# A GRU over 128 steps: step 0's products of r ahead of step 1's, the bias products in front of them, and one set of GpSimd's sums a step earlier

## The chip, the cores and the metric

The kernel runs on one core of a Trainium2 chip. The metric is the device time of one execution in microseconds (us), taken as the median of three runs. Beside it stands one profiled execution, whose trace gives the start and the end of every instruction; the span is the time from its first to its last instruction.

The engines go by these names in the profile: PE is TensorE (matmuls; PEld its weight loads), DVE is VectorE, ACT is ScalarE, POOL is GpSimd, SP is SyncE, which here issues transfers only. SPq, ACTq and POOLq are transfers issued by these three engines.

## The reference

A gated recurrent unit over x (64 sequences, 128 steps, 512 inputs), with a start state of 64 x 512, and the input added to its output. All in float32.

```
def step(h, inp):
    x_t, prop = inp
    comb = concatenate([x_t, h], axis=-1)
    z = sigmoid(comb @ Wz + bz)
    r = sigmoid(comb @ Wr + br)
    comb2 = concatenate([x_t, r * h], axis=-1)
    h_cand = tanh(comb2 @ Wh + bh)
    h_new = (1.0 - z) * h + z * h_cand
    h_next = where(prop, tanh(h_new @ Wp + bp), h_new)
    return (h_next, h_new)
# prop holds at every fourth step but the last
# out = x + the h_new of all steps
```

Each weight matrix of the gates has 1024 rows: the first 512 meet x (the input weights, `wx` in the kernel), the last 512 meet h (the recurrent weights, `wh`). Wp has 512 rows.

## The kernel before, in words

The 64 sequences are worked on in two halves of 32. The state lies with four column blocks of 128 side by side in the partitions (`NQ = 4`, `V = 32`). Every matmul of the kernel uses a 32-column strip of TensorE, so four of them run beside each other.

There are two kinds of product. The recurrent ones (`gate`, tiles `rec_0`, `rec_1`, `rec_z`) need the state of the step before: r first, then z, then the candidate with r * h, then at every fourth step the propagation with Wp. The input products do not depend on the state and are put into the gaps of the recurrence as a queue of units (`put`, `fill`). One unit of the plain kind (`plain_unit`) is one 128-row block `k` of x times one gate's input weights, for both halves: eight matmul instructions. From step 4 on the input products are formed for four steps at a time from sums and differences of x and of the weights (`batch`), which takes fewer products and leaves additions to VectorE and GpSimd. GpSimd forms the sums of the weights (`sum_outer`, `sum_inner`) in the first four steps and the sums of x (`sum_raw12`, `sum_s12`, `sum_raw4` and so on) all along, adds the parts of the results (`pair_left`, `outer_1`, ...), and adds the state to x for the output (line 803).

The order of the work on each engine is the order of the program text: it is written out by hand and no scheduler changes it. Two generators, one for each half, are interleaved by a count of columns (`LAG`, at the end of the kernel). Each engine works through its own instructions in order and waits for the others by semaphores. SyncE, ScalarE and GpSimd also issue transfers, and these stand in the order of that engine's other work. The transfers of SyncE and ScalarE share eight completion counters: a transfer that takes a counter first waits for the last one that held it.

The change concerns the start. Its order before is this:

- Loads: x of step 0 (four pieces on SyncE and ScalarE), r's input weights in two halves (`load_wx(R, 0, 2)`, `load_wx(R, 2, K)`, SyncE), between them x of step 1 (ScalarE) and the three bias rows (GpSimd's queue, line 132), then z's and the candidate's input weights (SyncE, 1 MB each), x of step 2, the start state (GpSimd's queue, behind a small copy that waits for r's weights).
- TensorE: 48 products of zeros (`idle(48)`); two units of r for step 0; two units of r for step 1; the bias products (`spread`: a row of ones times the bias rows, which ScalarE then copies into `bias_x`); the other two units of r for step 0 and for step 1; then the units of z, of the candidate, of step 2, and the recurrence of step 0 with r's recurrent weights.
- VectorE transposes x of a step (`join_x`) before that step's units; ScalarE issues half of the loads of r's recurrent weights (`load_wh(R)`) behind its three copies of the bias products.

Later, GpSimd has this order around steps 2 and 3: the bias and the sum of the first pair behind r of step 2 (`pair_left(0, 1, 2)`), the sums of x for the steps 8 to 11 (`sum_raw12`, `sum_s12`), line 803 of step 2, then behind r of step 3 `pair_right(0, 1, 10)` and the four operations of `sum_inner(7, ...)` (lines 319 to 322), then behind step 3 `pair_left(1, 8, 9)` and `pair_right(1, 8, 11)` and the sums that follow, up to `sum_raw4` (tile `s4r`, lines 330 to 333).

Of the kernel before, what the change touches and what calls it, by code (L numbers as in the profile page):

```python
# [18 lines left out]
def kernel(  # L19
# [14 lines left out]
    nc = tc.nc  # L34
# [13 lines left out]
    R, Z, H_ = range(3)  # L48
# [39 lines left out]
    def part(q):  # L88
        return slice(q * V, (q + 1) * V)
# [22 lines left out]
    def load_step(t, engs=both_queues):  # L112
        for q in (0, 2, 1, 3):
            engs[q // 2].dma_start(
                out=xr[0][part(q), t], in_=x[:, t, ts(q, J)].rearrange("(h b) u -> b h u", h=S)
            )

    def load_wx(i, k0, k1):
        nc.sync.dma_start(
            out=wx[:, k0:k1, i, :],  # L120
            in_=gates_in[i][:D].rearrange("(p k) n -> p k n", k=K)[:, k0:k1],
        )
# [3 lines left out]
    bias_p = const.tile([P, S, J], F32, name="bias_p")  # L126
    new_xr(0)
    load_step(0)
    load_wx(R, 0, 2)
    load_step(1, (nc.scalar, nc.scalar))  # L130
    for i, b in enumerate((br, bh, bz)):
        nc.gpsimd.dma_start(out=bias_row[:, i, :], in_=b.rearrange("(o n) -> o n", o=1))
# [17 lines left out]
    def load_wh(i):  # L150
        load_w(wh[i], gates_in[i][D:], engs=both_queues)
# [36 lines left out]
    def quarters(v):  # L188
        return v.rearrange("p n (d c j) -> p c n d j", d=2, c=2)

    def spread(bank, rows, which):
        bank = bank.rearrange("p (i d j) -> p i d j", i=2, d=2)
        for h in range(S):
            for c in range(2):
                nc.tensor.matmul(
                    bank[part(2 * h + c), 0 : len(which)],
                    lhsT=ones,
                    rhs=quarters(bias_row[:, rows])[:, c],
                    start=True,
                    stop=True,  # L200
                )
        for j, i in enumerate(which):
            nc.scalar.copy(
                bias_x[:, :, :, i, :].rearrange("p n d u -> p d n u"),
                bank[:, j].rearrange("p d (n u) -> p d n u", n=C),
            )
# [4 lines left out]
    def idle(n):  # L211
        for i in range(n):
            nc.tensor.matmul(
                rec[i // NQ % 3].rearrange("p a d n -> p (a d n)")[part(i % NQ)],
                lhsT=zeros[:, :V],
                rhs=zeros,
                start=True,
                stop=True,
            )
# [39 lines left out]
    def join_x(g, i):  # L259
        if g * Q4 >= T:  # L260
            return
        if g not in xT:
            xT[g] = xtp.tile([P, Q4, C, P], F32, tag="xT", name=f"xT_{g}")
        src = xr[g] if g < FIRST else xs[g]
        nc.vector.transpose(
            out=xT[g][:, i].rearrange("p c (a h b) -> p h (c a) b", a=S, h=S),
            in_=src[:, i].rearrange("p h (e k) -> p h k e", k=K),
        )
# [14 lines left out]
    def inner(i, ka, na):  # L283
        return OPERAND[i](ka)[:, :, :, ts(na, J // 4)]

    def leftover(i):
        return din[:, i - 1] if i <= 3 else inner(i, 0, 1)
# [25 lines left out]
    def sum_inner(i, eng, gates=slice(0, 3)):  # L313
        def of(v):
            return v[:, :, gates]

        t = [of(tt[:, i - 1, n]) for n in range(3)]
        v = {ab: of(inner(i, *ab)) for ab in ((0, 0), (0, 1), (1, 0), (1, 1))}
        eng.tensor_sub(t[1], v[1, 1], v[0, 1])
        eng.tensor_add(t[0], t[1], v[0, 0])  # L320
        eng.tensor_sub(t[2], v[1, 0], t[0])
        eng.tensor_sub(of(leftover(i)), v[0, 1], v[0, 0])
# [88 lines left out]
    def put(units):  # L411
        for unit, cols, bank, end, read in units:
            queue.append((unit, cols, reader.get(bank, -1), end))
            for b in read:
                reader[b] = len(queue) - 1
# [38 lines left out]
    def plain(t, gates=(R, Z, H_)):  # L454
        order = [(e, k) for e in gates for k in range(K)]
        if t == Q4 - 1:
            order = [(e, k) for k in range(K) for e in gates]
        return [
            plain_unit(
                t,  # L460
                e,
                k,
                k == 0,
                *((lambda: add_bias(t, gates), gates) if t > 1 and (e, k) == order[-1] else ()),
            )
            for e, k in order
        ]
# [101 lines left out]
    def add(dst, a, b):  # L569
        nc.gpsimd.tensor_add(dst, a, b)  # L570

    def with_bias(g, i, v):
        m = M[g, i].rearrange("p b d g u -> p b (d g u)")
        v = v.rearrange("p d g u -> p (d g u)")
        nc.gpsimd.tensor_add(m, m, v.unsqueeze(1).to_broadcast([P, 2, 3 * J]))  # L575

    def c_block(g, a, nb):
        new_cp(2 * g + a)
        return flat(cp[2 * g + a][:, nb])

    def m_(g, i):
        return flat(M[g, i])
# [17 lines left out]
    def outer_u2(g):  # L600
        add(m_(g, 7), m_(g, 7), m_(g, 6))
# [7 lines left out]
    def pair_left(a, p1, p2, g=1):  # L609
        with_bias(g, p2, bias0)  # L610
        add(c_block(g, a, 0), m_(g, p1), m_(g, p2))

    def pair_right(a, p1, x_, g=1):
        with_bias(g, x_, bias_x[:, 1])
        add(c_block(g, a, 1), m_(g, p1), m_(g, x_))
# [11 lines left out]
    def both(n):  # L627
        for _ in range(n):
            for h in range(S):
                for _ in fill(1, h):  # L630
                    pass

    def now(units):
        put(units)
        both(len(units))

    first = {i: [plain(t, (i,)) for t in range(2)] for i in (R, Z, H_)}
    idle(48)
    join_x(0, 0)
    now(first[R][0][:2])  # L640
    join_x(0, 1)
    now(first[R][1][:2])
    spread(scratch[3], slice(0, 2), (R, H_))
    spread(scratch[1], slice(2, 3), (Z,))
    nc.gpsimd.tensor_sub(bias_d, bias_x[:, 1], bias0)
    load_wh(R)
    now(first[R][0][2:] + first[R][1][2:])
    for t in range(2):
        add_bias(t, (R,))
    for h in range(S):  # L650
# [65 lines left out]
    def behind_r(t, duo, u):  # L716
        odd = FIRST + 2 * duo + 1
        if t == 2:
            pair_left(0, 1, 2)
        elif t == 3:  # L720
            pair_right(0, 1, 10)
            sum_inner(7, nc.gpsimd)
        if t == 4:
            sum_inner(4, nc.gpsimd)
        if u == 0 and duo >= 1 and odd - 2 < LAST:
            outer_u2(odd - 2)
# [101 lines left out]
    def half(h):  # L828

        for t in range(T):  # L830
# [10 lines left out]
            if h == 1:  # L841
                behind_r(t, duo, u)
# [129 lines left out]
```

## Time and profile before

| what | us |
|---|---|
| median of three runs | 1269.39 |
| lowest, highest | 1267.61, 1269.46 |
| the profiled execution's own time | 1266.3 |
| its span | 1264.5 |
| TensorE busy | 1250.6 |
| GpSimd busy | 891.1 |
| ScalarE busy | 835.2 |
| VectorE busy | 803.9 |

A row of the trace in order of time has the start in us, the duration, the engine, the line of the kernel, the operation, what it writes and reads, the shapes, how many instructions the row merges, and in brackets how long the engine stood idle before it and what ended that. Matmuls are pipelined, so the duration of one is longer than the distance to the next. A row of stretches has the bounds, the length, the busy time of PE, PEld, DVE, ACT and POOL with their counts, the clock that TensorE was granted as a share of the full one, the mean busy share of the DMA engines, and the GB/s that they moved. A row of transfers has KB each and the median us from issue to landing. Line numbers are those of the kernel before.

### The profile page before, as it was taken

What the parts mean: (1) busy time and instruction counts of PE and PEld (TensorE: products, weight loads), DVE (VectorE), ACT (ScalarE), POOL (GpSimd) and SP (SyncE); (2) the same over time, 40 slices, a digit from 0 to 9 for tenths busy, and PEclk for the clock granted to TensorE, in tenths of its full rate; (3) what the DMA queues carried; (4) which work ended last, traced back from release to release, by engine and by line L of the source; (5) the groups of instructions that cost most, each with busy time, mean ns of one, the idle gap of its engine ahead of it and who ended that gap; (6) DMA issues with size and microseconds to landing.
All of it is one profiled execution on the core that took longest, in us unless ns stands there. A gap on an engine that the chain in (4) does not pass through costs nothing.

```text
span 1264.5 us, 60718 instructions
## 1 busy us (share of the span) xinstructions
PE 1250.6 (99%) x25960; PEld 1161.0 (92%) x25960; DVE 803.9 (64%) x2165; ACT 835.2 (66%) x2685; POOL 891.1 (70%) x1032
## 2 busy tenths in 40 slices
PE   8999999999999999999999999999999999999997
PEld 4798899999999999999999999999999999999875
DVE  4665666666666666666666666666666666666544
ACT  1566666666666666666666666666666666667665
POOL 3899767777776778767778677777767787677530
PEclk9999999999999999999999999999999999999999
DMA  8301111111121110211111211111111111111010
GB/s 234 95 22 45 44 51 49 40 37 53 36 53 41 48 51 22 53 53 37 53 28 45 53 44 45 42 47 37 52 39 51 44 29 53 53 36 36 15 40 19
DMA packets 113172, 60.82 MB, mean 48 GB/s; under 512 B 12776, under 2 KB 109288, under 8 KB 112904
## 3 DMA queue, kind: packets, MB, share of 16 engines
q1 hardware_dynamic: 110532, 54.71, 16.3%
q8 instruction: 205, 3.36, 1.1%
q10 hardware_dynamic: 2116, 2.10, 0.7%
q14 instruction: 63, 0.52, 0.1%
q0 software_dynamic: 256, 0.14, 0.1%
HBM read 40.11 MB, written 16.78 MB: 45 GB/s over the span
## 4 chain that ended last, share of the span: by engine, by line
PE 94%; POOL 2%; issue 1%; DMA 1%; ACT 1%; DVE 1%; SPq 0%; ACTq 0%; POOLq 0%; DVEq 0%
PE rec L223 42%; PE rec_z L223 16%; PE scratch_r L223 13%; PE scratch_q L223 10%; PE scratch_a L223 5%; PE scratch_x L223 4%; PE scratch_y L223 4%; DMA xr<-in_x_dram 1%; POOL cp L570 1%; POOL mb L575 1%; ACT rec_z L249 0%; SPq L813 0%; POOL xr L803 0%; ACT c L249 0%; DVE rec_z L884 0%
## 5 line engine op out<-in xcount | busy, mean ns | idle before, releaser
L223 PE MATMUL rec<-wh,rhT 128*32 128x256 f32 x4096 | 375.1, 379 | 0.0
L223 PE MATMUL rec<-wh,hT 128*32 128x256 f32 x3072 | 281.2, 379 | 1.7 <-DVE hT L252 1.7
L223 PE MATMUL rec_z<-wh,hT 128*32 128x256 f32 x3072 | 281.5, 379 | 0.1
L223 PEld LDWEIGHTS rec<-wh,rhT 128*32 128x32 f32 x4096 | 249.6, 110 | 19.1 <-ACT scratch_r L249 0.5
L249 ACT ACTIVATE scratch_r<-rec 64x128 f32<-64x128 f32 x512 | 128.0, 250 | 133.9 <-PE rec L223 67.7
L399 ACT COPY rec<-cp 64x256 f32<-64x256 f32 x512 | 189.8, 371 | 21.5 <-DVE cp L437 2.0
L223 PEld LDWEIGHTS rec_z<-wh,hT 128*32 128x32 f32 x3072 | 192.1, 110 | 9.3 <-ACT rec_z L399 0.6
L223 PEld LDWEIGHTS rec<-wh,hT 128*32 128x32 f32 x3072 | 186.2, 110 | 14.6 <-ACT c L249 2.7
L249 ACT ACTIVATE rec_z<-rec_z 64x128 f32<-64x128 f32 x512 | 128.0, 250 | 97.8 <-PE rec_z L223 85.7
L249 ACT ACTIVATE c<-rec 64x128 f32<-64x128 f32 x512 | 138.9, 271 | 60.2 <-PE rec L223 48.8
L803 POOL TENSOR_TENSOR xr<-xr,h 128x256 f32<-128x256 f32 x127 | 92.9, 732 | 93.0 <-DVE h L893 93.0
L570 POOL TENSOR_TENSOR mb<-mb,mb 128x768 f32<-128x768 f32 x58 | 106.2, 1832 | 67.0 <-DVE mb L536 67.0
L570 POOL TENSOR_TENSOR cp<-mb,mb 128x768 f32<-128x768 f32 x76 | 139.0, 1829 | 8.1 <-DVE mb L536 4.4
L570 POOL TENSOR_TENSOR cp<-mb 128x768 f32<-128x768 f32 x46 | 84.3, 1832 | 56.8 <-ACT rec_z L399 55.4
L223 PE MATMUL scratch_r<-tw,s 128*32 128x192 f32 x928 | 120.9, 326 | 0.0
L509 ACT COPY cq<-scratch_q 128x384 f32<-128x384 f32 x212 | 102.0, 481 | 19.8 <-PE scratch_q L223 18.4
L526 DVE TENSOR_TENSOR cx<-scratch_r,cx 128x384 f32<-128x384 f32 x106 | 59.1, 557 | 85.8 <-PE scratch_r L223 67.9
L861 DVE SCALAR_TENSOR_TENSOR keep<-rec_z,h 128x256 f32<-128x256 f32 x96 | 40.7, 424 | 104.1 <-ACT rec_z L249 99.9
L223 PE MATMUL scratch_q<-tt,s 128*32 128x192 f32 x928 | 103.6, 326 | 0.0
L532 DVE TENSOR_TENSOR mb<-scratch_q,cx 128x384 f32<-128x384 f32 x106 | 59.0, 557 | 62.7 <-ACT cq L509 62.7
L845 DVE TENSOR_TENSOR rh<-scratch_r,h 128x128 f32<-128x128 f32 x192 | 56.0, 292 | 60.3 <-ACT scratch_r L249 60.3
L223 PE MATMUL rec<-wh,hpT 128*32 128x256 f32 x992 | 91.4, 379 | 0.1
(183 smaller groups left out, 3832.3 us busy)
## 6 DMA issues: line engine op xcount, KB each, us to landing
out_dram<-xr SPq DMA_DIRECT2D x249, 64.0 KB, 1.8
xr<-in_x_dram SPq DMA_DIRECT2D x248, 64.0 KB, 2.0
xs<-in_x_dram SPq DMA_DIRECT2D x240, 64.0 KB, 2.0
wx<-in_L_cond_Wr_dram SPq DMA_DIRECT2D x2, 512.0 KB, 5.0
wx<-in_L_cond_Wz_dram SPq DMA_DIRECT2D x1, 1024.0 KB, 7.1
wx<-in_L_cond_Wh_dram SPq DMA_DIRECT2D x1, 1024.0 KB, 8.2
wp<-in_L_cond_Wp_dram SPq DMA_DIRECT2D x4, 256.0 KB, 5.0
wh<-in_L_cond_Wr_dram SPq DMA_DIRECT2D x2, 256.0 KB, 9.9
```

The lines of the kernel that those rows point to most:

```text
L223: nc.tensor.matmul(ps[part(2 * h + c)], lhsT=left, rhs=rhs(c), start=start, stop=True, skip_group_check=True,)
L249: nc.scalar.activation(dst[ts(d, 2 * V)], gate_ps(i, h)[ts(h, 2 * V), d, :], func)
L399: nc.scalar.copy(gate_ps(i, h)[rows].rearrange("p d (c n) -> p d c n", c=C), G[t][rows, :, :, i, :].rearrange("p c d n -> p d c n"),)
L509: nc.scalar.copy(c[:, :nm], ps[:, :nm])
L526: nc.vector.tensor_add(T2[what][:, :nm], r_ps[:, :nm], T2[what][:, :nm])
L532: nc.vector.tensor_add(blocks(1, 1), runs(q_ps[:, :nm]), runs(T2[what][:, :nm]))
L570: nc.gpsimd.tensor_add(dst, a, b)
L575: nc.gpsimd.tensor_add(m, m, v.unsqueeze(1).to_broadcast([P, 2, 3 * J]))
L803: nc.gpsimd.tensor_add(xr[g][:, j], xr[g][:, j], h_new)
L845: nc.vector.tensor_mul(rh[:, h, :], r_, h_old[:, h, :])
L861: nc.vector.scalar_tensor_tensor(out=keep, in0=z, scalar=1.0, in1=h_old, op0=ALU.subtract, op1=ALU.mult)
```

## The change

In the loads, r's input weights come in three pieces instead of two: the first row block, the second, and the last two together. In TensorE's order there are 36 products of zeros instead of 48; the bias products come right behind them, ahead of all units of r; then come the four units of r for step 0, then the four for step 1. The loads of r's recurrent weights and GpSimd's `bias_d` stand between these two groups in the text. On GpSimd, the four operations of `sum_inner(7, ...)` stand behind r of step 2 instead of step 3. No operation other than the twelve products of zeros is removed, and the order on VectorE is the same as before.

```diff
     load_step(0)
-    load_wx(R, 0, 2)
+    load_wx(R, 0, 1)
+    load_wx(R, 1, 2)
     load_step(1, (nc.scalar, nc.scalar))
...
-    idle(48)
-    join_x(0, 0)
-    now(first[R][0][:2])
-    join_x(0, 1)
-    now(first[R][1][:2])
+    idle(36)
     spread(scratch[3], slice(0, 2), (R, H_))
     spread(scratch[1], slice(2, 3), (Z,))
+    join_x(0, 0)
+    now(first[R][0])
+    join_x(0, 1)
     nc.gpsimd.tensor_sub(bias_d, bias_x[:, 1], bias0)
     load_wh(R)
-    now(first[R][0][2:] + first[R][1][2:])
+    now(first[R][1])
...
         if t == 2:
             pair_left(0, 1, 2)
+            sum_inner(7, nc.gpsimd)
         elif t == 3:
             pair_right(0, 1, 10)
-            sum_inner(7, nc.gpsimd)
```

## The prediction

> **What bounds the kernel now.** I read the busy times first, then TensorE's start in order of time, its clock by stretches, the loads, and last GpSimd around the one wait of TensorE between start and end that is over 1 us.
>
> From the page:
> ```profile
> span 1264.5 us, 60718 instructions
> PE 1250.6 (99%) x25960; PEld 1161.0 (92%) x25960; DVE 803.9 (64%) x2165; ACT 835.2 (66%) x2685; POOL 891.1 (70%) x1032
> ```
> TensorE is busy for 1250.6 of 1264.5 us. An edit pays only where TensorE stands still or runs at a lower clock, and that is some fifteen microseconds in all.
>
> Its start in order of time (start, us, engine and line, what, count, [idle before, and what ended it]):
> ```profile
> 5.24 0.39 PE L213 MATMUL rec_z<-zeros 128*32 128x512 bf16 x4
> 6.83 1.07 PE L223 MATMUL scratch_q<-wx,xT 128*32 128x256 f32 x16 [1.20 <-DMA wx<-in_L_cond_Wr_dram]
> 9.38 1.07 PE L223 MATMUL scratch_a<-wx,xT 128*32 128x256 f32 x16 [1.49 <-DVE xT L265]
> 10.39 1.06 PE L195 MATMUL scratch_x<-tt,ones 1*32 1x512 f32 x8
> 11.27 0.94 PE L195 MATMUL scratch_r<-tt,ones 1*32 1x256 f32 x8
> ...
> 15.20 1.90 PE L223 MATMUL scratch_q<-wx,xT 128*32 128x256 f32 x32
> 16.93 1.90 PE L223 MATMUL scratch_a<-wx,xT 128*32 128x256 f32 x32
> 18.65 1.90 PE L223 MATMUL scratch_r<-wx,xT 128*32 128x256 f32 x32
> ```
> ```profile
> 24.70 1.93 PE L223 MATMUL rec<-wh,hT_init 128*32 128x256 f32 x28
> ```
> r's first units run at 6.83, after 1.20 of waiting for r's input weights; step 1's at 9.38, after 1.49 for its transposed x; z's at 15.20, the candidate's at 18.65, the recurrence from 24.70. From 15.20 to 16.93 32 instructions take 1.73 us: 0.43 per unit of 8 at full clock, so r's eight units are 3.45. The bias products are 0.88 (10.39 to 11.27) for the rows of 512 columns, so 0.44 for as many of 256: 1.32 together. What follows them is slower, and the stretches say why (PE, PEld, DVE, ACT, POOL busy, then the granted clock, DMA share, GB/s):
> ```profile
> 4.59:8.01 3.42, 2.11 (x36) 0.81 (x28) 0.87 (x1) 0.51 (x2) 0.00 (x0) 1.00 1.03 357
> 8.01:11.42 3.41, 2.04 (x28) 0.82 (x32) 0.63 (x1) 0.00 (x0) 1.52 (x3) 1.00 1.03 348
> 11.42:14.83 3.41, 3.41 (x40) 1.32 (x32) 0.42 (x1) 1.18 (x4) 0.99 (x1) 0.50 1.08 312
> ```
> ```profile
> 1257.28:1260.70 3.42, 1.33 (x20) 0.47 (x8) 1.60 (x5) 1.78 (x7) 0.72 (x1) 1.00 0.08 19
> 1260.70:1264.50 3.80, 0.00 (x0) 0.00 (x0) 0.00 (x0) 0.00 (x0) 0.00 (x0) 0.50 0.13 35
> ```
> From 11.42 to 14.83 the clock is 0.50: 1.7 us lost. The stretch before it was busy for 2.04 us; the one at the end that also precedes 0.50 for 1.33; the one that kept the clock for 2.11.
>
> **The change, part by part.**
>
> Fewer warm-up products. Twelve of 48 go. At the 0.43 us for eight that r's units show, twelve are 0.65, so they now end near 5.0 instead of 5.6 (5.24 + 0.39). Nothing waits for them, but the stretch from 4.59 to 8.01 becomes emptier, which comes below.
>
> Bias products first. They wait for the bias rows, which GpSimd's queue loads (issues, then KB each and us from issue to landing):
> ```profile
> 1.96 0.51 POOL L132 DMA_DIRECT2D tt<-in_L_cond_bh_dram  x1
> 2.46 0.48 POOL L132 DMA_DIRECT2D tt<-in_L_cond_bz_dram  x1
> ```
> ```profile
> tt<-in_L_cond_bh_dram POOLq DMA_DIRECT2D x1, 2.0 KB, 4.9
> tt<-in_L_cond_bz_dram POOLq DMA_DIRECT2D x1, 2.0 KB, 4.9
> ```
> Landings at 6.9 and 7.4. At 10.39 nobody noticed; now TensorE starts with them, at 6.9, and the wait for r's weights is replaced by one for the bias rows of the same length.
>
> The clock. From 4.59 to 8.01 the new kernel is busy for some 0.4 (warm-up) and 1.1 (from 6.9): 1.5 us, near the 1.33 that was followed by 0.50. So I take half clock from 8.01 to 11.42, in place of 11.42 to 14.83: the loss of 1.7 us moves and stays.
>
> r's units. The work ahead of z is 1.32 + 3.45 = 4.77, plus 1.7 for the clock: 6.9 + 6.5 = 13.4; with the 0.2 that the same sum misses today (9.38 + 3.9 + 1.7 = 15.0 against 15.20) z begins at 13.6, 1.6 us earlier. Step 1's x, ready by 9.38, is needed only near 11.7, so that wait of 1.5 is covered; if it were not, it would cost again what it costs now.
>
> The loads (SyncE's and ScalarE's issues; then us to landing):
> ```profile
> 4.60 0.66 SPq L119 DMA_DIRECT2D wx<-in_L_cond_Wz_dram  x1
> 8.31 0.54 SPq L119 DMA_DIRECT2D wx<-in_L_cond_Wh_dram  x1
> 12.26 0.80 ACTq L100 DMA_DIRECT2D wh<-in_L_cond_Wr_dram  x2
> ```
> ```profile
> wx<-in_L_cond_Wz_dram SPq DMA_DIRECT2D x1, 1024.0 KB, 7.1
> wx<-in_L_cond_Wh_dram SPq DMA_DIRECT2D x1, 1024.0 KB, 8.2
> ```
> ```profile
> wh<-in_L_cond_Wr_dram ACTq DMA_DIRECT2D x2, 256.0 KB, 9.6
> ```
> z's input weights land at 4.60 + 7.1 = 11.7, the candidate's at 8.31 + 8.2 = 16.5, r's recurrent ones by 12.26 + 0.4 + 9.6 = 22.3. One more load on SyncE is 0.4 us of issue there (half of 0.80 for two on ScalarE). It also shifts who waits for whom, since each load waits for an earlier one that held its completion counter: the last of r's three (half the weights) now waits where z's does today, until 4.60, and z's follows at 5.1. The engines are at a share of 1.03 in that stretch, so a later issue is mostly hidden behind packets already queued; I put 0 to 0.5 us on z's landing, 12.0, still before 13.6. The candidate's load waits for another piece of step 1's x: 8.7 in place of 8.31. The two loads of r's recurrent weights on SyncE now wait for z's landing and go out near 12.0; from there the same loads took ScalarE's queue 9.6 us, so 21.6 to 22.0, and they are needed at 24.70 less the gain, 23.6: covered. Those on ScalarE stand behind the three copies of the bias products, which now end near 9: issued at 9 instead of 12.26, into the time in which the candidate's weights move.
>
> Here lies the term that decides. TensorE could start the candidate at 13.6 + 3.45 = 17.0; the weights landed at 16.5 before. Rates around it:
> ```profile
> 9.00:13.00 4.00, 3.62 (x42) 1.23 (x46) 0.33 (x1) 1.02 (x3) 1.52 (x3) 0.80 1.03 359
> 13.00:16.00 3.00, 3.00 (x44) 1.57 (x40) 0.97 (x3) 0.74 (x2) 0.70 (x1) 0.69 1.11 206
> ```
> ScalarE's two loads are 0.52 MB. None of it ahead of the candidate's last byte: 16.5, no wait. All of it, at 206 GB/s: 2.5 us later, 19.0. I take the lower third, 0.8 us, since SyncE's own pair now stays out of that time: 17.3, so the candidate starts at 17.5 instead of 18.65. The start gains 1.1 us, between 1.6 and -0.4. Everything behind it shifts along, as long as GpSimd's own chain keeps up.
>
> GpSimd's sums. Four operations leave the place behind step 3's r for step 2's:
> ```profile
> 62.38 0.46 POOL L330 TENSOR_TENSOR s12r<-xT 128x128 f32<-128x128 f32 x1 [4.74 <-PE scratch_r L223]
> ...
> 71.96 1.00 POOL L319 TENSOR_TENSOR tt<-tw 128x384 f32<-128x384 f32 x1
> ...
> 76.07 1.84 POOL L575 TENSOR_TENSOR mb<-mb,bias_x 128x768 f32<-128x768 f32 x1
> ...
> 103.89 0.32 POOL L332 TENSOR_TENSOR s4r<-xT 128x64 f32<-128x64 f32 x1
> ```
> ```profile
> 73.89 0.55 DVE L536 TENSOR_TENSOR mb<-scratch_x,cq 128x384 f32<-128x384 f32 x1
> ```
> ```profile
> 102.83 0.36 PE L223 MATMUL scratch_a<-wx,xT 128*32 128x192 f32 x2
> 104.26 0.36 PE L223 MATMUL scratch_x<-tt,s4r 128*32 128x192 f32 x2 [1.07 <-POOL s4r L332]
> ```
> ```profile
> 62.38:104.21 41.83, 40.81 (x870) 37.43 (x862) 26.41 (x70) 25.80 (x82) 40.49 (x46) 1.00 0.17 41
> ```
> They last from 71.96 to 76.07, 4.1 us, and go into the hole of 4.74 before 62.38, where GpSimd waits for TensorE anyway. Behind 62.38 GpSimd is busy to s4r without a pause worth the name (busy for 40.49 of 41.83 us in the last row), so s4r could come 4.1 us earlier; but the addition at 76.07 then waits for VectorE's mb, done at 74.44. The lead that counts is 76.07 - 74.44 = 1.6: s4r is ready at 104.21 - 1.6 = 102.6, and TensorE asks for it at 102.9. The stall, 104.26 - 102.83 less a pitch of about 0.1, is 1.3 us and goes, with 0.3 to spare. Were the hole gone, the same operations would stand in the same queue ahead of s4r: no loss and no gain. I take 1.3, between 0 and 1.4.
>
> Sum: 1.1 + 1.3 = 2.4 us. Against the profiled execution's 1266.3 us that is 1263.9. The median of the runs, 1269.4, is 3.1 above that execution; I carry the difference over: 1267.0 us. What a measurement can tell from no change is 0.2%, 2.5 us, so this lies just inside.
>
> **Rivals.**
>
> No wait for the candidate's weights (they land at 16.5 as before): the start gains 1.6, in all 2.9, 1266.5.
>
> The weights are later by far, and the kernel slower. ScalarE's loads of r's recurrent weights took 9.6 us, and the rate fell to 206 GB/s while such loads ran. If that rate holds for all that lies ahead, the candidate's load is 0.4 (issue) + 2.5 (0.52 MB ahead) + 2.2 (its 1.05 MB at 206 instead of 359) later: 21.6. Then the candidate starts at 21.8, 3.1 us later than today, and less the 1.3 of s4r the kernel takes 1271.2. At 22.3, the landing of r's recurrent weights today, it would be 1271.9. It is slower than before from a landing at 19.7 on. For it speaks that 206; against it, that SyncE's pair has left the stretch. The Trainium skill (DMA: Bandwidth & Descriptors, Issuing engines are not separate DMA queues) states that loads of all queues run on the same 16 engines and interleave, by which an earlier issue on ScalarE is paid for by the other loads; shares of 1.03 to 1.11 agree.
>
> The clock keeps its full rate. If only a stretch without any work lowers it, the gap from 5.0 to 6.9 is too short and the 1.7 us are not lost: z would start at 11.9, so behind its landing, at 12.2, and end at 15.7, and the candidate is bound by its weights alone. Landing at 16.5, they let it start at 16.7, 1.95 us earlier, with s4r 3.2 in all, 1266.2; each microsecond that they land sooner, now that SyncE's pair is out of the way, gives another, down to 15.7. The Trainium skill (TensorE: Matmul & The Clock Gate, Part 1) states just that rule, half rate after at least one idle window of about 3.4 us. The row 8.01:11.42, 2.04 us busy and yet followed by 0.50, speaks against it.
>
> A second stretch at half clock. The one-row bias products may hardly count as work: 8.01:11.42 held them and was followed by 0.50, while 4.59:8.01, as busy without them, was not. With other edges of the stretches they could keep the clock down twice: 1.7 more, the start loses 0.6, 1268.7.
>
> The moved sums do nothing, because mb's time binds more than its row says: 1268.3.
>
> **Numbers.** Forecast 0.42; no wait for the weights 0.16; weights far later 0.20; full clock 0.07; second half-clock stretch 0.09; sums without effect 0.06. The range goes from 1264.8, the full clock with weights over a microsecond sooner, to 1271.0, the late weights. Faster by over 0.2%, below 1266.9: no wait, full clock and a third of the forecast, 0.37. Slower, above 1271.9: two thirds of the late weights, since no row bounds their landing from above, 0.13. Within: 0.50.
>
> **What would show it.** Right: the first real product of TensorE at 6.9 on bias rows, a stretch at 0.50 that begins earlier, z's units near 13.6, the candidate's behind a wait on its weights near 17.5, GpSimd's four sums before 62 and no wait on s4r. Wrong: the candidate's units after 18.65; s4r still waited for; bias rows later than 7.5, which nothing covers any more.

## The result and the profile after

The changed kernel takes 1269.09 us in the median of 22 runs (1266.0 to 1271.51). The kernel before, run beside it 22 times, takes 1265.38 (1264.25 to 1269.59); the three runs given above, 1267.61 to 1269.46, lie at the upper end of that. The ratio is 1.0023, with a 95% interval from 1.0015 to 1.0031: slower, by some 3 to 4 us, where a faster kernel or no change was forecast. The profiled executions are further apart: 1271.51 against 1266.3 us of own time, spans of 1269.6 and 1264.5.

From the page of the changed kernel:
```profile
span 1269.6 us, 60695 instructions
PE 1254.7 (99%) x25948; PEld 1167.5 (92%) x25948; DVE 804.4 (63%) x2165; ACT 835.8 (66%) x2685; POOL 892.1 (70%) x1032
```
TensorE is busy for 4.1 us longer with twelve instructions fewer. Busy time that grows without work is a lower clock, so the 5.1 us of span are partly that. Its start in order of time (columns as above; the line numbers are one higher than before):
```profile
4.59 0.64 PE L214 MATMUL rec_z<-zeros 128*32 128x512 bf16 x4
5.65 1.93 PE L196 MATMUL scratch_x<-tt,ones 1*32 1x512 f32 x8 [0.42 <-DMA tt<-in_L_cond_bh_dram]
7.33 1.10 PE L196 MATMUL scratch_r<-tt,ones 1*32 1x256 f32 x8
8.36 4.00 PE L224 MATMUL scratch_q<-wx,xT 128*32 128x256 f32 x32
12.13 2.81 PE L224 MATMUL scratch_a<-wx,xT 128*32 128x256 f32 x32
14.77 1.90 PE L224 MATMUL scratch_q<-wx,xT 128*32 128x256 f32 x32
16.50 1.90 PE L224 MATMUL scratch_a<-wx,xT 128*32 128x256 f32 x32
22.71 3.64 PE L224 MATMUL scratch_r<-wx,xT 128*32 128x256 f32 x32 [4.31 <-DMA wx<-in_L_cond_Wh_dram]
26.10 2.67 PE L224 MATMUL scratch_x<-wx,xT 128*32 128x256 f32 x32
31.18 1.94 PE L224 MATMUL rec<-wh,hT_init 128*32 128x256 f32 x28
```
z's units begin at 14.77, 0.4 us earlier than before. Then TensorE stands for 4.31 us: the candidate's input weights are not there. Its units begin at 22.71 instead of 18.65, and they are slow: 3.39 us from 22.71 to 26.10, where a step's units took 1.73 (16.50 - 14.77). So the recurrence begins at 31.18 instead of 24.70, 6.5 us later. What follows it is shorter: 1269.6 - 31.18 = 1238.4 us, against 1264.5 - 24.70 = 1239.8. These 1.4 us are the sums' gain; the start lost 6.5.

The clock by stretches (columns as above):
```profile
0.32:3.73 3.41, 2.53 (x24) 0.93 (x28) 0.27 (x1) 0.10 (x1) 1.88 (x8) 1.00 0.34 84
3.73:7.15 3.42, 3.00 (x24) 0.76 (x20) 0.92 (x2) 1.38 (x2) 0.00 (x0) 1.00 0.84 224
7.15:10.56 3.41, 3.29 (x32) 0.95 (x28) 0.36 (x1) 0.92 (x3) 0.13 (x2) 1.00 0.96 349
10.56:13.97 3.41, 3.41 (x36) 1.57 (x38) 0.42 (x1) 0.74 (x2) 2.41 (x4) 1.00 1.07 352
13.97:17.39 3.42, 3.42 (x72) 1.89 (x68) 2.28 (x6) 0.00 (x0) 0.00 (x0) 1.00 1.11 196
17.39:20.80 3.41, 1.01 (x20) 0.34 (x12) 1.85 (x5) 0.38 (x1) 0.00 (x0) 1.00 1.01 171
20.80:24.22 3.42, 1.51 (x16) 0.90 (x20) 2.18 (x8) 0.00 (x0) 0.00 (x0) 0.50 0.62 151
24.22:27.63 3.41, 3.41 (x36) 1.80 (x32) 1.33 (x5) 0.00 (x0) 0.00 (x0) 0.50 0.94 237
```
Two stretches in a row, 20.80 to 27.63, are at 0.50: the wait left 1.01 us of work in the stretch ahead of the first and 1.51 in the stretch ahead of the second. The first four rows show 1.00, but there the column is not to be trusted: 32 and 36 instructions fill the last two stretches ahead of 13.97, 72 the one behind it. TensorE ran at half rate from its first instruction to 13.97.

What the loads did (ScalarE's and SyncE's issues in order of time, then the mean share of the DMA engines and GB/s as the last two columns of stretches):
```profile
6.81 0.54 SPq L119 DMA_DIRECT2D wx<-in_L_cond_Wh_dram  x1
8.78 0.40 ACTq L100 DMA_DIRECT2D wh<-in_L_cond_Wr_dram  x1
10.40 0.32 ACTq L100 DMA_DIRECT2D wh<-in_L_cond_Wr_dram  x1
```
```profile
9.00:13.00 4.00, 3.88 (x42) 1.40 (x34) 0.42 (x1) 0.67 (x4) 2.47 (x4) 1.00 1.05 384
16.00:20.00 4.00, 2.40 (x48) 1.08 (x36) 3.19 (x9) 0.38 (x1) 0.00 (x0) 1.00 1.08 177
20.00:24.00 4.00, 1.29 (x14) 0.71 (x17) 1.96 (x7) 0.00 (x0) 0.00 (x0) 0.60 0.66 144
```
The candidate's load went out 1.5 us earlier than before (8.31) and was waited for until 22.71. ScalarE's two loads of r's recurrent weights went out at 8.78 and 10.40 instead of 12.26. From 16 to 20 the DMA engines are as fully occupied as from 9 to 13, but move 177 GB/s instead of 384. Full engines at half the bytes: whatever is moved ahead of the candidate's last byte takes twice the time there.

GpSimd around the sums:
```profile
63.55 1.01 POOL L320 TENSOR_TENSOR tt<-tw 128x384 f32<-128x384 f32 x1
...
68.86 0.46 POOL L331 TENSOR_TENSOR s12r<-xT 128x128 f32<-128x128 f32 x1 [1.16 <-PE scratch_r L224]
...
81.00 1.82 POOL L576 TENSOR_TENSOR mb<-mb,bias_x 128x768 f32<-128x768 f32 x1 [2.51 <-DVE mb L537]
...
108.83 0.32 POOL L333 TENSOR_TENSOR s4r<-xT 128x64 f32<-128x64 f32 x1
```
The four operations fill the hole ahead of `s12r`, of which 1.16 us are left; GpSimd then waits for `mb`, 2.51 us; the operation on `s4r` for which TensorE waited before (line 332 there, 333 here) ends at 109.15, that is 77.97 after the recurrence began, against 79.51 before. TensorE's wait for it is gone.

### The profile page after: what moved, and what is told of

The parts are those of the page before. It is cut to its first block, busy times and chain, and to the rows that moved or that the text cites. A ratio compares the mean times of both kernels' runs of the same rounds, so it can differ in the third digit from the quotient of the medians.

```text
span 1269.6 us, 60695 instructions
## 1 busy us (share of the span) xinstructions
PE 1254.7 (99%) x25948; PEld 1167.5 (92%) x25948; DVE 804.4 (63%) x2165; ACT 835.8 (66%) x2685; POOL 892.1 (70%) x1032
## 4 chain that ended last, share of the span: by engine, by line
PE 96%; DMA 2%; ACT 1%; issue 1%; DVE 1%; POOLq 0%; POOL 0%; ACTq 0%; DVEq 0%
PE rec L224 44%; PE rec_z L224 16%; PE scratch_r L224 14%; PE scratch_q L224 10%; PE scratch_a L224 5%; PE scratch_x L224 4%; PE scratch_y L224 4%; DMA wx<-in_L_cond_Wh_dram 1%; DMA xr<-in_x_dram 0%; ACT rec_z L250 0%; ACT c L250 0%; DVE rec_z L884 0%; DVE h L893 0%; DVE hT L253 0%; POOLq L967 0%
```

## The experiments

Two theories were to be told apart. One: ScalarE's recurrent loads, freed by the earlier bias products, take the DMA engines from the candidate's weights, and the wait costs again by the clock. The other: something else of the change does it, namely the third load and the counters that it shifts, or the clock at the start. "Candidate" is the start of its units, "recurrence" that of the first recurrent product, "rest" the span behind it.

| kernel | ScalarE's recurrent loads | candidate (wait) | recurrence | rest | median, us | ratio to before (95%) |
|---|---|---|---|---|---|---|
| before | 12.26 | 18.65 | 24.70 | 1239.8 | 1265.38 | |
| changed | 8.78, 10.40 | 22.71 (4.31) | 31.18 | 1238.4 | 1269.09 | 1.0023 (1.0015 to 1.0031) |
| before, recurrent loads early | 8.04 | 21.40 (4.49) | 29.62 | 1239.8 | 1271.34 | 1.0033 (1.0020 to 1.0045) |
| before, sums moved | 11.84, 12.26 | 16.90 | 22.94 | 1239.2 | 1264.97 | 0.9993 (0.9982 to 1.0004) |
| before, three loads | 10.76, 12.70 | 17.61 | 24.27 | 1239.8 | 1266.87 | 1.0005 (0.9991 to 1.0019) |
| changed, recurrent loads late | 12.69 | 18.42 (0.20) | 24.46 | 1238.8 | 1264.85 | 0.9984 (0.9972 to 0.9996) |
| changed, 48 warm-ups | 7.66, 9.17 | 21.40 (4.95) | 29.61 | 1238.4 | 1269.33 | 1.0015 (1.0003 to 1.0027) |
| changed, late and 48 | 11.67, 12.52 | 17.60 (0.35) | 23.64 | 1238.5 | 1267.13 | 0.9995 (0.9981 to 1.0008) |
| changed, wait filled | 8.66, 10.44 | 22.48 (0) | 28.53 | 1238.4 | 1268.51 | 1.0011 (1.0003 to 1.0020) |
| changed, two loads | 9.85 | 22.63 (4.16) | 30.36 | 1238.3 | 1266.73 | 1.0005 (0.9992 to 1.0018) |
| changed, two loads and late | 13.71 | 18.55 (0) | 24.59 | 1238.4 | 1264.78 | 0.9979 (0.9969 to 0.9989) |
| the same, 48 and filled | 11.56 | 17.36 (1.23) | 23.40 | 1238.6 | 1265.45 | 0.9981 (0.9971 to 0.9991) |

The starts and rests come from one traced execution each, the medians from 11 to 22; each ratio is to runs of the kernel before on the same chip, whose medians ranged from 1265.4 to 1267.7, so kernels are compared by the ratios.

**The suspected cause alone.** The kernel before, with one call moved:

```diff
+    load_wh(R)
     spread(scratch[3], slice(0, 2), (R, H_))
     spread(scratch[1], slice(2, 3), (Z,))
     nc.gpsimd.tensor_sub(bias_d, bias_x[:, 1], bias0)
-    load_wh(R)
```

> The kernel before, with one edit: ScalarE issues its two loads of r's recurrent weights ahead of its copies of the bias products, so near 8.8 instead of 12.26. Theory (early recurrent loads hold back the candidate's input weights): these land at 20 to 22.6 instead of 16.5, the candidate's units start there instead of at 18.65 behind a wait of 2 us or more, and with the half clock that follows such a wait the kernel is 3 to 6 us slower than before. Rival (the three loads, or the new order on TensorE, are at fault): landing near 16.5, candidate at 18.65, within 0.7 us of before.

```profile
8.04 0.81 ACTq L100 DMA_DIRECT2D wh<-in_L_cond_Wr_dram  x2
```
```profile
21.40 3.64 PE L223 MATMUL scratch_r<-wx,xT 128*32 128x256 f32 x32 [4.49 <-DMA wx<-in_L_cond_Wh_dram]
...
29.62 1.94 PE L223 MATMUL rec<-wh,hT_init 128*32 128x256 f32 x28
```
```profile
9.00:13.00 4.00, 3.90 (x60) 1.76 (x64) 0.31 (x2) 0.92 (x3) 1.54 (x3) 1.00 1.10 264
```
The issue of ScalarE's loads is at 8.04, the wait is 4.49, and the kernel is 0.33% slower. By the ratio that is the whole of the changed kernel's loss and what the moved sums give back there (0.23% and some 0.1%), without its order, its three loads or its 36 products. From 9 to 13 much the same occupancy (1.10 against 1.03) now moves 264 GB/s, where the kernel before moved 359. The trace also tells the queues apart (packets, MB, share of the 16 engines' time). q10 moves 2.10 MB in the whole span, as much as all of ScalarE's loads; q1 is SyncE's. From 9 to 13, in the kernel before:
```profile
q1 hardware_dynamic: 673, 1.34, 93.9%
q10 hardware_dynamic: 240, 0.10, 9.0%
```
and with the early loads:
```profile
q10 hardware_dynamic: 518, 0.61, 73.7%
q1 hardware_dynamic: 216, 0.41, 31.3%
```
ScalarE's pair, 0.52 MB, is moved in that time, and SyncE's queue, on which the candidate's weights come, moves 0.93 MB less. The theory stands. The changed kernel shows the same a little later: from 13 to 17 ScalarE's queue moves 0.47 MB and SyncE's 0.32, in the kernel before 0.02 and 0.64.

**The cause taken out of the changed kernel.**

```diff
-    load_wh(R)
     now(first[R][1])
     for t in range(2):
         add_bias(t, (R,))
     for h in range(S):
         seed(R, 0, h)
+    load_wh(R)
```

> The changed kernel, with one edit: the loads of r's recurrent weights stand behind the first two seeds in the text, so ScalarE issues its two near 13.4 instead of 8.78 and 10.40. Theory (early recurrent loads): the candidate's input weights land at 16.5 to 17.5 instead of 22.58, no wait for them over 0.5 us, candidate's units near 18.2; TensorE still runs at half rate to about 14, since only 36 warm-up products stand in front. In all 1 to 2 us faster than the kernel before. Rival (the three loads shift the completion counters): the landing stays above 20, and the kernel stays 2.5 us or more slower than before.

```profile
18.42 1.93 PE L224 MATMUL scratch_r<-wx,xT 128*32 128x256 f32 x32 [0.20 <-DMA wx<-in_L_cond_Wh_dram]
...
24.46 1.96 PE L224 MATMUL rec<-wh,hT_init 128*32 128x256 f32 x28
```
The wait falls from 4.31 to 0.20 us, and the kernel is faster than before by 0.16%. All other parts of the change are still in it, so none of them makes the loss without the early loads. Its 12 runs lie between 1263.92 and 1265.84, far closer together than those of the kernel before.

**The clock at the start.** `idle(36)` is `idle(48)` again, in the changed kernel, and together with the late loads:

> The changed kernel with the 48 warm-up products of before instead of 36. Theory (a full stretch of work is what brings the full clock, and 36 products leave a gap ahead of the bias products): no gap at 5.2, full rate from about 7.2 to 8 instead of 13.97, r's eight units done by 12.5 and z's units bound by their weights (landing 13.55). But the candidate's weights still land near 22.6, so the wait for them only grows to 5 us or more, and the time stays within 1 us of the changed kernel. Rival (the clock at the start is the main loss): 3 us faster than the changed kernel, so no slower than before.

```profile
5.91 1.06 PE L196 MATMUL scratch_x<-tt,ones 1*32 1x512 f32 x8
...
12.79 1.93 PE L224 MATMUL scratch_q<-wx,xT 128*32 128x256 f32 x32 [0.80 <-DMA wx<-in_L_cond_Wz_dram]
...
21.40 3.64 PE L224 MATMUL scratch_r<-wx,xT 128*32 128x256 f32 x32 [4.95 <-DMA wx<-in_L_cond_Wh_dram]
```
With 48 the full rate is there from 5.91 (1.06 us for the eight bias products instead of 1.93), and the units of z are 2 us earlier. In this execution the candidate's weights also came 1.3 us earlier, and the wait grew to 4.95. 1.0015 against the changed kernel's 1.0023: no difference that these intervals can tell. So the half rate to 13.97 costs little, if anything, while weights bound the start. In the kernel before, it was this stretch, filled with work, that brought the full rate:
```profile
1.18:4.59 3.41, 3.39 (x33) 1.29 (x37) 0.00 (x0) 0.98 (x1) 1.62 (x3) 1.00 0.59 131
```
How long TensorE is busy in a stretch does not decide by itself. 3.29 of 3.41 us did not bring the full rate in the changed kernel, and 2.80 did in the kernel before with three loads (0.59 to 4.00). The clock fell after 2.90 us of work in the changed kernel with late loads and 48 products (6.12 to 9.53), and stayed after 1.73 in the kernel before with early loads (5.33 to 8.74). What decides was not found.

> The changed kernel with both edits: r's recurrent loads behind the first two seeds, and 48 warm-up products. Theory (two causes, the loads first and the clock behind them): z's units near 13.6, candidate's near 17.3 with a wait under 0.5 us, no stretch at half clock after the warm-up, and with the 1.3 us of s4r 2 to 3.5 us faster than before; faster than the late loads alone by about 1 us. Rival (the clock plays no part once the weights come in time): same as the late loads alone within 0.4 us.

The execution seen has the starts that were expected (candidate 17.60, recurrence 23.64, the lowest run of the twelve), though with a stretch at half clock, from 9.54 to 12.95, that was not. The median is not as expected either: 0.9995, no gain over before, and less than the late loads alone. Two further executions of it:

> The kernel with late recurrent loads and 48 warm-up products once more, to see an execution near its median of 1267.1 us; the one seen took 1263.8 and began its recurrence at 23.64. Theory (the spread is the clock's: where the edges of the stretches of 3.4 us fall, a stretch with gaps for r's and z's weights is followed by one at half clock): an execution of over 1266 us shows one or two stretches at half clock after 10 us, its recurrence begins 2 us or more later, and what follows that is 1238.5 us as in the others. Rival (the loads' landings vary): the candidate's wait for its weights is over 2 us, with no stretch at half clock ahead of it.

> The same kernel again, for the same question and with the same expectations: slower by stretches at half clock, or by a later landing of the candidate's weights.

```profile
10.29 1.93 PE L224 MATMUL scratch_q<-wx,xT 128*32 128x256 f32 x16 [1.64 <-DMA wx<-in_L_cond_Wr_dram]
11.99 3.64 PE L224 MATMUL scratch_a<-wx,xT 128*32 128x256 f32 x32
...
25.22 1.93 PE L224 MATMUL rec<-wh,hT_init 128*32 128x256 f32 x28
```
They took 1264.39 and 1265.39 us. The third is shown: at full rate TensorE reaches the end of r's first weights sooner, waits 1.64 for the last load of r, and step 1's units then take 3.42 us instead of 1.73. The recurrence begins at 25.22, 1.6 later than in the first execution. The other one had a wait of 1.87 for the candidate's weights and no half clock. So both theories for the spread hold in part; no traced execution took over 1266 us, so the 2.3 us between the two medians stay unexplained to that extent.

**What the wait costs by the clock.** In the changed kernel, 80 products of zeros ahead of the candidate's units (`idle` takes the bank as an argument):

```diff
+    idle(80, scratch[4])
     now(sum(first[H_], []))
```

> The changed kernel with 80 more products of zeros (about 4.3 us at full rate) between z's units and the candidate's, into a bank that nothing uses yet, so that TensorE works through its wait for the candidate's weights. Theory (the wait costs twice: 4.1 us of delay, and about 2.4 us by the half clock that follows it): the candidate's units start near 22.7 as in the changed kernel, but take 1.73 us for each step instead of 3.39 and 2.49; the recurrence begins near 28.8 instead of 31.18; 1.5 to 2.5 us faster than the changed kernel, within 2 us of before on the slower side. Rival (the half clock has another cause, or hits later work): the recurrence begins at 31 or later, no faster than the changed kernel.

```profile
18.17 4.49 PE L214 MATMUL scratch_y<-zeros 128*32 128x512 bf16 x80
22.48 1.90 PE L224 MATMUL scratch_r<-wx,xT 128*32 128x256 f32 x32
24.21 1.90 PE L224 MATMUL scratch_x<-wx,xT 128*32 128x256 f32 x32
```
The candidate comes at nearly the same time (22.48 against 22.71), but at full rate, and the recurrence begins at 28.53 instead of 31.18. From the candidate's first unit to the recurrence it is 6.05 us, as in the kernel before (24.70 - 18.65), where the changed kernel took 8.47. So of the 6.5 us lost at the start 2.4 are the clock's and 4.1 the delay (22.71 - 18.65). In the five other executions that waited, the same stretch of work took 7.45 to 8.22 us, so there the clock cost 1.4 to 2.2. By the ratios the filling gains 1.5 us (1.0011 against 1.0023), the lower end of what was expected; the two intervals overlap.

**The third load.** The kernel before with three loads, and the changed kernel with two (the two lines of `load_wx` exchanged):

> The kernel before, with r's input weights in three loads and nothing else. Theory (one more load costs 0.4 us of issue and shifts two waits for counters, all of it covered): the candidate's weights land between 16.5 and 17.5, candidate's units at 18.65 or up to 0.3 us off, within 0.5 us of before. Rival (the third load, held to a landing of x, is what makes the weights late): the last of r's weights lands at 10 or later, the candidate's at 18.7 or later, 1 us or more slower.

> The changed kernel with r's input weights in two loads, as before, instead of three. Theory (the third load has no part in it): the candidate's units still start at 21 or later behind a wait of 2.5 us or more, time within 1 us of the changed kernel. Rival (the third load, which waits for a landing of x, is half of the loss): candidate at 19.5 or earlier, 2 us or more faster than the changed kernel.

In the kernel before, three loads make no difference that can be told (1.0005, with 1 inside), and the candidate came at 17.61 without a wait. In the changed kernel with two loads it waits as long as with three:
```profile
7.00 1.93 PE L195 MATMUL scratch_x<-tt,ones 1*32 1x512 f32 x8 [1.77 <-DMA tt<-in_L_cond_bh_dram]
...
22.63 3.00 PE L223 MATMUL scratch_r<-wx,xT 128*32 128x256 f32 x32 [4.16 <-DMA wx<-in_L_cond_Wh_dram]
...
30.36 1.96 PE L223 MATMUL rec<-wh,hT_init 128*32 128x256 f32 x28
```
But its twelve runs fall into groups, four near 1264.8, four from 1266.1 to 1267.0, four from 1269.6 to 1270.5, and this execution is of the last. Two further executions of it, and one of the kernel before:

> The changed kernel with two loads for r's input weights, a second execution. Theory (the lateness hangs on when ScalarE's recurrent loads go out against the candidate's): an execution below 1267 us shows the candidate's units near 18 to 20 and ScalarE's loads issued later than 9.85, or the candidate's load issued earlier than 8.92. Rival (the clock alone makes the groups): the candidate's units at 22 or later as in the one seen, with fewer stretches at half clock.

> A third execution of the same kernel, for the same question: the group of its time goes with the landing of the candidate's weights (theory) or with the stretches at half clock only (rival).

> The kernel before, a second execution; the one shown took 1266.3 us, with one stretch at half clock and the recurrence from 24.70. Theory (its spread is the clock's): an execution near 1264.4 us has no stretch at half clock behind the warm-up and begins its recurrence near 22.9; one near 1269.5 has two or more, and begins near 28; the candidate's weights land at 16 to 17 in either. Rival (landings vary): the candidate's units wait for their weights.

Both executions of the two-load kernel took 1269.3 to 1269.5 us and show the same again: loads issued at 9.29 and 9.12, candidate at 21.45 and 21.37 behind waits of 2.77 and 3.92. No traced execution was without the wait, so what differs in those eight runs, and whether the third load makes the lateness more regular, stays open. The kernel before took 1266.55, with the candidate at 18.77 and the recurrence at 24.81, like the one shown above:
```profile
8.69 1.09 SPq L100 DMA_DIRECT2D wh<-in_L_cond_Wr_dram  x2
...
12.32 0.86 ACTq L100 DMA_DIRECT2D wh<-in_L_cond_Wr_dram  x2
```
Here is a second thing to see: SyncE's own pair of r's recurrent loads, as large as ScalarE's, goes out at 8.69, right behind the candidate's load. In the ten executions with late loads on ScalarE it goes out at 8.69 to 10.26, in the seven with early ones only at 11.54 to 13.64, since it then waits for z's input weights to land. So no run moves ScalarE's pair by itself; the two pairs change places, and the candidate's weights are late where ScalarE's comes first. What SyncE's pair costs where it comes first is not shown, since no run is without it.

**With two loads and late loads:**

> The changed kernel with the late recurrent loads and with two loads for r's input weights. Theory (third load without a part): the same as the late loads alone, 1263.9 to 1265.8 us, candidate's units near 18.4. Rival (third load costs): candidate by 17.9, 0.5 to 1 us faster than the late loads alone.

The same as with three, as the theory had it: 1263.54 to 1265.21, 0.9979, the fastest version by its ratio. It beats the kernel before by 0.2% and the changed one by more.

**With fuller stretches.** To the last kernel, 48 products in front, and `idle(16, scratch[4])` between the first two and the last two units of r for step 0:

> The late recurrent loads, two loads for r's input weights, 48 warm-up products, and 16 more products of zeros between the first two and the last two units of r for step 0, so that TensorE works through its wait for the second half of r's weights. Theory (a stretch with gaps is what lowers the clock): full rate from 5 to 8 us on and kept; z's units at 12 to 13, candidate's at 17 to 18 bound by their weights, recurrence at 23 to 24; 1.5 to 3 us faster than before in the median, and a narrower spread than with 48 products alone (1263.8 to 1268.7). Rival (the spread is not from the gap for r's weights): as wide a spread as there, and a median of 1266 or more.

```profile
17.36 1.93 PE L223 MATMUL scratch_r<-wx,xT 128*32 128x256 f32 x32 [1.23 <-DMA wx<-in_L_cond_Wh_dram]
...
23.40 1.96 PE L223 MATMUL rec<-wh,hT_init 128*32 128x256 f32 x28
```
The runs spread over 2.8 us (1263.64 to 1266.43) where 48 products alone had 4.9, so work in the gap may help against the spread; the two kernels also differ in the third load. The ratio, 0.9981, is that of the version without it: TensorE is now early and the candidate's weights bound the start, with 1.23 us of waiting.

**The sums alone.** The kernel before with `sum_inner(7, nc.gpsimd)` behind `pair_left(0, 1, 2)`:

> The kernel before, with GpSimd's four operations of the sums moved to step 2 and nothing else. Theory (the sum predicted at 1.3 us is right and stands by itself): the wait of TensorE for s4r falls from 1.07 us to 0.3 or less, the time from the first recurrent product of step 0 to the end of the span falls from 1239.8 to 1238.4 us, the start is as before; 1.0 to 1.4 us faster than before. Rival (what waits for VectorE's mb binds): the wait stays at 0.8 or more, within 0.4 us of before.

TensorE's products wait 0.06 us for `s4r` instead of 1.07, as expected, but the weight load ahead of them still waits 0.4 us, where it waited 1.4. The span is 1262.1 us, 2.4 less than before, of which 1.8 lie in a start at full clock, which the edit does not touch, and 0.6 in the rest: 1239.2 where 1238.4 was expected. `s4r` still sets the time here: it comes 78.89 us after the recurrence began, 0.6 earlier than before and not 1.5 as in the changed kernel. The recurrence begins 1.8 us earlier than before, but GpSimd's chain ahead of the hole only 0.2 (its addition on line 575 at 53.70 instead of 53.91). So the four operations fill more than the hole: `s12r` begins without a wait at 61.50, 38.56 after the recurrence began, instead of 37.68. By the ratio, 0.9993, the gain is 0.9 us, and the interval holds 1.

## Why the prediction was wrong

The step that failed is the one it called the term that decides: the landing of the candidate's input weights. It put 0.8 us on ScalarE's earlier loads, a lower third between 0 and 2.5 us, and the candidate at 17.5. It started at 22.71, behind a wait of 4.31. The bound itself was wrong, not only the place in it: it counted ScalarE's bytes ahead of the candidate's at 206 GB/s and left the candidate's own at the rate of the undisturbed kernel. The late-weights rival counted both and came to 21.8, within 1 us of what happened. It was given 0.20. In part that nearness is luck. Both sums use the 206 GB/s of the kernel before from 13 to 16, and no byte of ScalarE's loads was moved there: SyncE's queue moved 0.49 MB and GpSimd's, with the start state, 0.12.

The argument for the lower third was that SyncE's pair had left the stretch. It had not. It went out at 13.57, 9 us before the weights were there. SyncE's issues up to and including the candidate's weights are 3.21 MB, and by 22.6 its queue had moved 3.89. In the kernel before it had moved 3.73 by 16.5, when the weights landed, so there too as much as the pair was moved from behind them before they were there. What changed is that ScalarE's pair was moved in that time as well. The Trainium skill (DMA: Bandwidth & Descriptors, Rules for kernel authors), on which the prediction did not draw here, says of two transfers to disjoint halves of the partitions that they use the same ring on each DMA engine if one engine issues them, and packet-interleaved rings if two do. The trace agrees for ScalarE's pair, which takes 0.47 of the 0.87 MB from 13 to 17 while the candidate's weights are on their way. For SyncE's pair it shows no order between the two loads as a whole.

Over the seventeen executions with a trace: where the first of ScalarE's two loads went out by 9.85, the candidate waited 2.8 to 5.0 us, in all six (a seventh hides the wait behind products of zeros); where it went out at 10.76 or later, at most 1.9, in all ten. No run put all four loads on SyncE, so the ring itself was not tested. Why the engines move only half the bytes while these loads run stays open too.

Point by point:

- *Warm-up ends at 5.0, nothing waits.* It ended at 5.23. Harmless, but the rate behind the 0.65 us was that of a full clock, which this execution did not have.
- *Bias rows land at 6.9.* They were there by 5.65, with three loads; in three traced executions of the kernel with two, TensorE waited for them until 6.82 to 7.29. The prediction did not see that the third load might bear on this; why it does was not tested.
- *Half clock from 8.01 to 11.42, 1.7 us lost as before.* Wrong in form. TensorE was at half rate from the start to 13.97. The edges of the stretches lie elsewhere in each execution: at 1.18 and 4.59 in the one of before, where the 48 products filled a stretch (3.39 of 3.41 us) and the full clock came at 4.59; at 0.32 and 3.73 here, where 2.53, 3.00 and 3.29 us of work did not bring it and 3.41 did. The Trainium skill (TensorE: Matmul & The Clock Gate, Part 1) states that these windows run freely and do not start with the kernel; the two traces agree. How full a stretch is does not decide alone either (2.80 us brought the full rate in another run). An argument from the edges of one execution says little of the next.
- *z at 13.6.* 14.77, for that reason.
- *A second stretch at half clock,* a rival with 0.09 and 1.7 us: it came, but from the wait for the candidate's weights, two stretches and 2.4 us. The late-weights rival lacked this: it priced the delay, 3.1 us at the start, and not the clock that a wait takes along.
- *r's recurrent weights are covered.* Right: no wait at the recurrence in any of these kernels.
- *The sums bring 1.3 us.* Right for the changed kernel: the rest of the span is 1.4 shorter, GpSimd waits for `mb` as worked out, and `s4r` came 1.5 earlier in the recurrence's time where 1.6 was put. Its condition, that GpSimd's own chain keeps up, matters: in the run with the sums alone it did not hold, and 0.6 was left.
- *The level.* The prediction carried over the three runs' median, 1269.39; over 22 runs the kernel before has 1265.38. That is no error in the change's cost, but it alone put the forecast 4 us high, and the measured 1269.09 lies inside the range only by that luck. The top of the range, 1271.0, also lies below the prediction's own sums for the late weights, 1271.2 and 1271.9.

The sum as measured in the two traces: +4.1 for the delay, +2.4 for the clock, -1.4 for the sums, 5.1 us of span. It had been -1.1 and -1.3.

## What to carry to other kernels

A load that another engine issues earlier isn't free because it is needed later: before letting it go, look which load under way is needed first, and price it with that load's remaining bytes at the lower rate too, not with the newcomer's bytes alone. A wait of several microseconds on TensorE has a second price behind it, the half clock over the next stretches, here 2.4 us on 4.1. And where a kernel's runs spread over 5 us, one trace shows one draw of the clock's edges: judge a start by what binds it in any of them, here the landing of weights.

## What was not expected of the hardware

DMA engines at an occupancy of 1.08 moved 177 GB/s, and 384 at 1.05 some microseconds before, in one execution of the changed kernel. In the kernel before with early recurrent loads, occupancy 1.10 came with 264 GB/s against 359 in the same stretch of the kernel before. The occupancy tells that the engines are taken, not what they deliver.

A half-rate start was the steadier one. The late-load kernels with 36 products run at half rate to about 14 us, wait little, and spread over less than 2 us; with 48 products alone and the full clock early, TensorE runs into waits for weights, the runs spread over 4.9 us, and the ratio to before, 0.9995, shows no gain. The granted clock showed 1.00 in those first stretches, against 36 instructions in a stretch where full rate had 72.
